# Softmax of the node scores: from TensorE transposes to VectorE's 32x32 blocks, with some steps of the pattern moved

## The chip, the core and the metric

The kernel runs on one core of a Trainium2 chip. A core has TensorE (PE in the profile: matmuls, which take a 128-row weight tile and stream the other operand through it, into PSUM), VectorE (DVE), ScalarE (ACT), GpSimd (POOL) and SyncE (SP, which here only issues DMAs). Each engine works through its own queue in the order in which the program wrote it, and waits at an instruction until the semaphores it needs have been counted up. The metric is the device time of one execution in microseconds, lower is better.

## The reference, cut to what matters

64 graphs of 256 nodes with 512 features. Layer 0 is three graph convolutions, layer 1 one graph attention whose softmax runs over the 256 nodes of a graph; both end in a residual and a layer norm.

```python
# layer 0
def gcn(x, adj, W, b):
    return einsum('bnm,bmh->bnh', adj, einsum('bnf,fh->bnh', x, W)) + b
h = relu(gcn(x, adj, W1, b1)); h = relu(gcn(h, adj, W2, b2))
x = layernorm(x + gcn(h, adj, W3, b3))
# layer 1
q, k = split(x @ Wqk); v = x @ Wv
agg = einsum('bij,bjd->bid', adj, k * mask)
w = mask * sum(q * agg, -1) / sqrt(512)      # one score per node, [64, 256]
out = layernorm(x + softmax(w, axis=1)[:, :, None] * v)
```

All inputs and outputs are float32.

## The kernel before

The 64 graphs are worked on in 32 pairs (G = 2 graphs). The 256 nodes lie as NH = 2 halves of 128 partitions. Most matrix products are cut into 2x2 blocks and done in seven block products in place of eight; the generator `seven` (L110) issues them. It uses three PSUM banks: x takes product 1, is copied out by ScalarE (L118), takes product 6 on top, is copied again (L127), takes product 5 on top, is read by the add `c22`, and takes product 3 on top, which `c12` reads. Banks v and y take products 7 and 4, and 2; they are read by ScalarE (L132) and the adds `c21` and `c11`. Those adds are VectorE's `add` (L65), whose second operand is one of the copies. The sums and differences of blocks that feed the products are formed by GpSimd (`padd`, L68; `a_sums`, L275; `t_sums`, L350) or VectorE.

Six generators issue the work of a round of the outer loop, each for another pair:

- F (`front`): three times `support` (times W1, W2, W3, matmuls on L304) and twice `aggregate` (times the adjacency, L326, with relu on ScalarE, L329).
- S (`sums`): GpSimd's block sums for the next pair, the bias added to x (`x<-x,b3b`), and the four block sums of the adjacency (`aS`).
- B (`back`): the third aggregation (`adj_times`, L362), residual and layer norm of layer 0. It starts with `t_sums`, GpSimd's four sums of the blocks that the last `support` left (`T<-sup`, `T<-sup,T`).
- G (`gather`): adjacency times the masked result (L362).
- M (`attention`): the scores, from products against a matrix that is formed once from Wq, Wk and Wv (L542). The operand `ring` is fetched anew from memory for every pair, seven blocks ahead. `results(g)` ends a graph: two scores on VectorE (L559, one for each half of the nodes: a product with the gathered rows, summed into one column of `w`), and a sum `v<-R`. `results(1)` comes before the last products of M, `results(0)` after them.
- E (`finish`): the softmax (`softmax_rows`, `softmax_cols`), the weighted residual (L600), statistics and layer norm, and the store.

In what order the generators are stepped stands written out: a letter of ORDER is one step of that generator. START and LAST do so for the first and the last pair, END for what is left after it; in END, X and Y are E for the last pair, graph by graph. All engines' queues follow from this one order. At each step an engine's instructions are put behind what is already in its queue.

The softmax before: the scores `w` are [128, 2, 2], nodes on partitions. TensorE transposes both halves into one bank, [2, 256] (L381); VectorE takes the maximum (L383), ScalarE the exponential with its sum (L386), VectorE the reciprocal and the scaling (L388, L389). In E's second step TensorE transposes back (L396), VectorE copies to SBUF (L398), and four operations form residual plus softmax times v (L600). The scale 1/sqrt(512) is in `mask_s`, which the scores use.

Of the kernel before, what the change touches and what calls it, by code (L numbers as in the profile page):

```python
# [9 lines left out]
FP = mybir.dt.float32  # L10
AF = mybir.ActivationFunctionType
OP = mybir.AluOpType
AX = mybir.AxisListType

P = 128
PAIR = 2
G = PAIR
# [3 lines left out]
def gcn_then_graph_attention(ctx: ExitStack, tc: tile.TileContext, xT, xN, adjT, mask, W1, b1, W2, b2, W3, b3,  # L21
# [18 lines left out]
    nc = tc.nc  # L40
    NPAIR = xT.shape[0]
    N, D = 256, 512
    NH, DC = N // P, D // P
    HD = D // 2
    EPS = 1e-5
    ISCALE = 1.0 / math.sqrt(D)
    KEYS = ("T1", "T2", "T3", "T4")

    const = ctx.enter_context(tc.tile_pool(name="const", bufs=1))
    pool = ctx.enter_context(tc.tile_pool(name="work", bufs=1))  # L50
    small = ctx.enter_context(tc.tile_pool(name="small", bufs=2))
# [6 lines left out]
    def bank(shape=(P, G, N)):  # L58
        return psum.tile(list(shape), FP, name="ps", tag="ps")
# [110 lines left out]
    ident = const.tile([P, P], FP, name="ident")  # L170
# [16 lines left out]
    for n, b in ((1, b1), (2, b2)):  # L187
        t = const.tile([P, DC], FP, name=f"b{n}")
# [1 line left out]
        bcol.append(t)  # L190
    b3b = const.tile([P, D], FP, name="b3b")
    mask_t = const.tile([P, NH, NPAIR * G], FP, name="mask_t")
    mask_s = const.tile([P, NH, NPAIR * G], FP, name="mask_s")
    eps = const.tile([P, 1], FP, name="eps")
    nc.vector.memset(eps, EPS)

    def prepare():

        for n, w in ((2, W2), (3, W3)):
            begin, end = load_w(w, n)  # L200
            begin()
            yield from end()
        aTs[1] = load_adj(1)
        nc.sync.dma_start(b3b, b3.partition_broadcast(P))
        nc.sync.dma_start(mask_t, mask.rearrange("p (h b) -> p h b", h=NH))
        yield
        nc.vector.tensor_scalar(mask_s, mask_t, ISCALE, None, op0=OP.mult)
        yield from make_m()


# [6 lines left out]
    for k in STEPS:  # L217
        q = "abcd".index(k)
# [154 lines left out]
        nc.vector.scalar_tensor_tensor(nb, mvt[:, :, :, 0], -1.0, rs, op0=OP.mult, op1=OP.mult)  # L373
        return rs, nb

    def softmax_rows(w, gs):

        n = len(gs)
        pw = bank((n, N))
        for h in range(NH):  # L380
            nc.tensor.transpose(pw[:, h * P:(h + 1) * P], w[:, h, gs[0]:gs[0] + n], ident)  # L381
        nmax = small.tile([n, 1], FP, name="nmax")
        nc.vector.tensor_reduce(nmax, pw, AX.X, OP.max, negate=True)  # L383
        e = small.tile([n, N], FP, name="e", bufs=1)
        tot = small.tile([n, 1], FP, name="tot")
        nc.scalar.activation(e, pw, AF.Exp, bias=nmax, accum_out=tot)  # L386
        rtot = small.tile([n, 1], FP, name="rtot")
        nc.vector.reciprocal(rtot, tot)  # L388
        nc.vector.tensor_scalar(e, e, rtot, None, op0=OP.mult)  # L389
        return e  # L390

    def softmax_cols(sm, gs):
        n = len(gs)
        ps = bank((P, NH, n))
        for h in range(NH):
            nc.tensor.transpose(ps[:, h, :], sm[:, h * P:(h + 1) * P], ident[:n, :n])  # L396
        s = small.tile([P, NH, n], FP, name="s", bufs=2)
        nc.vector.tensor_copy(s, ps)  # L398
        return s


# [25 lines left out]
    def back(i, C, aS, x, end, put):  # L427
# [20 lines left out]
        b = i * G  # L448
# [56 lines left out]
                        aTs[i + 2] = load_adj(i + 2)  # L505
                yield
        put["G"] = gather()
        w = small.tile([P, NH, G], FP, name="w", bufs=2)
        put["M"] = attention(i, x1b, w, r, put)

    def attention(i, x1b, w, r, put):

        half = lambda n, s: pool.tile([P, 4 - s, 4, P], FP, name=n, tag=f"{n}{'ab'[s]}", bufs=1)
        Z = [half("Z", s) for s in range(2)]
        I = [pool.tile([P, 4, 4 - s, P], FP, name="I", tag=f"I{'ab'[s]}", bufs=1) for s in range(2)]
        zo = lambda o: Z[o // 4][:, o % 4]
        z = lambda n: zo(place[n]).rearrange("p (c g) n -> p c g n", c=2)
        sub = OP.subtract
        for n, b in ((1, x1b(0, 0)), (2, x1b(0, 1)), (4, x1b(1, 1))):
            nc.scalar.copy(z(n), b)  # L520
        for o, a, b, op in ((z(5), x1b(1, 0), x1b(1, 1), OP.add), (z(6), z(5), z(1), sub), (z(7), z(1), x1b(1, 0), sub),
                            (z(3), z(2), z(6), sub)):
            nc.vector.tensor_tensor(o, a, b, op=op)  # L523
        yield
        for s in range(2):
            padd(I[s][:, 2], Z[s][:, :, 0], Z[s][:, :, 1], sub)
            padd(I[s][:, 0], Z[s][:, :, 1], Z[s][:, :, 3])
            padd(I[s][:, 1], I[s][:, 0], Z[s][:, :, 0], sub)
            padd(I[s][:, 3], Z[s][:, :, 2], I[s][:, 1], sub)
            yield  # L530
        left = {n: (lambda o, k=k: zo(o)[:, k]) for n, k in ((1, 0), (2, 2), (4, 3))}
        left.update({n: (lambda o, k=k: I[o // 4][:, k, o % 4]) for n, k in ((5, 0), (6, 1), (7, 2), (3, 3))})
        at = [i * len(uses)]

        def inner(q, R, more=None):

            outer = OUTER[q]

            def mm(n, ps, first):
                wt = ring.pop(at[0])  # L540
                for k, o in enumerate(outer):
                    nc.tensor.matmul(ps[:, k], lhsT=left[n](place[o]), rhs=wt[:, k], start=(first and k == 0),  # L542
                                     stop=(k == len(outer) - 1), skip_group_check=True)
                fetch(at[0] + RING)
                at[0] += 1
            if more is None:
                c12, plus = lambda x: nc.scalar.copy(R[:, :, 0, 1], x), None
            else:
                c12 = lambda x: add(R[:, :, 0, 1], x, more[:, :, 0, 1])
                plus = (more[:, :, 0, 0], more[:, :, 1, 0], more[:, :, 1, 1])  # L550
            return seven(mm, (P, len(outer), HD), lambda y, t: add(R[:, :, 0, 0], y, t), c12,
                         lambda v, t: add(R[:, :, 1, 0], v, t), lambda v, t: add(R[:, :, 1, 1], v, t), plus=plus)
        v = pool.tile([P, G, NH, D], FP, name="v", tag="v", bufs=1)
        flat = lambda R: R.rearrange("p g j f -> p g (j f)")

        def score(R, h, g):
            t = put["gt"][:, h, g, :]
            b = i * G + g
            nc.vector.scalar_tensor_tensor(t, R[:, g].rearrange("p j f -> p (j f)"), mask_s[:, h, b:b + 1], t,  # L559
                                           op0=OP.mult, op1=OP.mult, accum_out=w[:, h, g:g + 1])  # L560

        def results(g):

            score(C[:, 0], 1, g)
            yield
            score(B[:, 0], 0, g)
            yield
            add(v[:, g, 1], flat(C[:, 0])[:, g], flat(C[:, 1])[:, g])
            put[g] = r, v, w
            yield  # L570

        R = {k: pool.tile([P, 2, G, 2, HD], FP, name="R", tag=t, bufs=1) for k, t in (("a", "T"), ("b", "x1T"))}
        A, B = R["a"], R["b"]
        run = {k: inner("ab".index(k), R[k]) for k in "ab"}
        for n, k in enumerate(STEPS):
            if n == 14:
                add(B[:, 0], B[:, 0], A[:, 0])
                yield
                nc.vector.tensor_tensor(B[:, 0], B[:, 0], B[:, 1], op=sub)  # L579
                yield  # L580
                add(v[:, :, 0], flat(A[:, 0]), flat(A[:, 1]))
                yield
                C = pool.tile([P, 2, G, 2, HD], FP, name="R", tag="Za", bufs=1)
                run.update(c=inner(2, C, B), d=inner(3, B[:, :1], B[:, :1]))
            if n == 26:
                yield from results(1)
            next(run[k])
            yield
        yield from results(0)

    def finish(i, prev, gs=range(G)):

        r, v, w = prev
        n = len(gs)
        sm = softmax_rows(w, gs)
        yield
        s = softmax_cols(sm, gs)
        for k, g in enumerate(gs):
            for h in range(NH):
                nc.vector.scalar_tensor_tensor(v[:, g, h], v[:, g, h], s[:, h, k:k + 1], r[:, g, h, :],  # L600
                                               op0=OP.mult, op1=OP.add)
        yield
        st = small.tile([P, NH, n, 6], FP, name="st")
# [10 lines left out]
        for k, g in enumerate(gs):  # L614
            for h in range(NH):
# [4 lines left out]

    ORDER = ("BFEFFFEBFBEFBBBFBBFBBFFFBFBESBEFBBGFFGEFEEGEGFFEFESFFGMMGSFEMGMMFMMMMMMMMMMMMMMMMMFM"
             "MMMMMSFMMMSSMMSMSSFMFSMFMMEMSMMFM")
    START = ("FBBFBFFFBBFBBBFBBFBBBBFBFFBBBBBBFBBFBBBBBBBBFFFFBBFBBBBBBFFBBSBFFBFBBSFBBBFFSBBBFSBB"
             "BBSBFBSBFBSSSSBSBBBSBBB")
    LAST = ("BFEFFFEBFBEFBBBFBBFBBFFFBFBESBEFBBGFFGEFEEGEGFFEFESFFGMMGSFEMGMMFMMMMMMMMMMMMMMMMMFM"
            "MMMMMSFMMMSSMMSMSSFMFSMFMMEMSMMFM")
    END = ("EEBEBEBEEBBBEEEBBBEEBBBBBBGMGMGBGMMBMEMMMMMGGMMMBMMMMGMMMMMMMMMMMMMMMMMMXMXMMMMXMMYM"
           "XMXXMXMYMYYYXXYYMMXXMYXYYYY")  # L630

    def run(order, rest, **gens):
        res = {}
# [77 lines left out]
```

## Time and profile before

| | |
|---|---|
| median of 3 runs | 2789.59 us (2786.75 to 2791.51) |
| the profiled execution's own time | 2780.69 us |
| its span, from first to last instruction | 2778.9 us |
| granted TensorE clock | 0.994 |
| busy: TensorE / weight loads / VectorE / ScalarE / GpSimd | 98 / 86 / 62 / 41 / 65 % of the span |
| L381, first transposes on TensorE | 66 matmuls, 13.0 us busy |
| L396, transposes back | 66 matmuls, 9.4 us busy |
| L383, L388, L389, L398 on VectorE | 33 of each; 412, 151, 1206, 151 ns mean |
| L386 exponential on ScalarE | 33; 465 ns mean, and 185 for its sum |
| L559 scores on VectorE | 128; 1425 ns mean, 740 to 1747 |

Times in a profile line are microseconds unless ns is written. In the timeline, a line is a start, a duration, engine, source line, operation, output<-inputs, their shapes and how many were merged; in brackets the idle time before it and what ended it. Durations of matmuls overlap, since they are pipelined; the distance between starts is what they cost. The same is true in part for VectorE: the next operation is shown to start some 0.08 us before the end of the one before. The time of an operation includes a wait for the memory ports. The listing by line gives for each operation the minimum, median and maximum in ns, and the first and last start.

### The profile page before, as it was taken

How to read it: one execution, taken by the hardware profiler on the slowest of the kernel's cores; microseconds unless marked ns; L12 is line 12 of the kernel's file. 1: busy time of each engine (PE TensorE's matmuls, PEld its weight loads, DVE VectorE, ACT ScalarE, POOL GpSimd, SP SyncE). 2: the span in 40 equal slices, each digit the busy share in tenths (PEclk: the TensorE clock that was granted, in tenths of full speed). 3: DMA queues.
4: the chain of work that ended last, by engine and by line, in shares of the span. 5: the costliest groups of instructions: out<-in, count | busy, mean ns of one | idle time of the engine just before them, and what ended most of it. 6: DMA issues, size and time to landing. Idle time of an engine off the chain costs nothing.

```text
span 2778.9 us, 37024 instructions
## 1 busy us (share of the span) xinstructions
PE 2731.4 (98%) x12688; PEld 2377.9 (86%) x12688; DVE 1723.4 (62%) x2900; ACT 1143.7 (41%) x1890; POOL 1795.9 (65%) x1446
## 2 busy tenths in 40 slices
PE   9999999999999999999999999999999999999996
PEld 8888888888888888888888888888888888888875
DVE  4566565665566665656666666655566655666666
ACT  3334344434444433444334444334443334443434
POOL 3666765676756666656667666767566676667663
PEclk9999999999999999999999999999999999999997
DMA  6444554344554345543445543455444455434442
GB/s 223 153 122 131 163 174 136 113 146 150 162 166 130 118 139 169 161 148 125 134 139 161 171 134 116 139 161 161 154 126 127 139 161 173 137 112 145 139 153 97
DMA packets 197752, 403.45 MB, mean 145 GB/s; under 512 B 20160, under 2 KB 57408, under 8 KB 189504
## 3 DMA queue, kind: packets, MB, share of 16 engines
q1 hardware_dynamic: 197568, 401.10, 45.8%
q8 instruction: 103, 1.69, 0.3%
q14 instruction: 81, 0.66, 0.1%
HBM read 328.54 MB, written 72.48 MB: 144 GB/s over the span
## 4 chain that ended last, share of the span: by engine, by line
PE 93%; DMA 3%; DVE 2%; issue 1%; POOL 1%; ACT 0%; SPq 0%; POOLq 0%; ACTq 0%; DVEq 0%
PE ps L304 41%; PE ps L542 22%; PE ps L326 16%; PE ps L362 14%; DMA ring<-mv 3%; PE ps L246 1%; DVE v L600 0%; DVE gt L559 0%; PE ps L381 0%; PE ps L396 0%; DMA xT<-in_xT 0%; DVE R L65 0%; POOL S L286 0%; POOL tmp L68 0%; DVE st L607 0%
## 5 line engine op out<-in xcount | busy, mean ns | idle before, releaser
L304 PE MATMUL ps<-w_T,S 128*128 128x256 f32 x2304 | 539.7, 379 | 3.8 <-POOL S L287 2.8
L304 PEld LDWEIGHTS ps<-w_T,S 128*128 128x128 f32 x2304 | 435.1, 190 | 63.9 <-POOL S L287 4.0
L326 PE MATMUL ps<-aT,sup 128*128 128x256 f32 x2048 | 457.7, 379 | 0.0
L65 DVE TENSOR_TENSOR R<-ps,tmp 128x512 f32<-128x512 f32 (+1 forms) x384 | 230.5, 622 | 365.5 <-PE ps L542 350.3
L542 PE MATMUL ps<-ring,I 128*128 128x256 f32 x1792 | 428.5, 381 | 13.3 <-DMA ring<-mv 13.1
L326 PEld LDWEIGHTS ps<-aT,sup 128*128 128x128 f32 x2048 | 389.0, 190 | 52.8
L283 POOL TENSOR_TENSOR S<-hT 128x512 f32<-128x512 f32 x64 | 81.7, 1277 | 492.1 <-ACT hT L329 492.1
L542 PEld LDWEIGHTS ps<-ring,I 128*128 128x128 f32 x1792 | 339.7, 190 | 64.7 <-issue 15.1
L127 ACT COPY tmp<-ps 128x512 f32<-128x512 f32 (+1 forms) x288 | 158.0, 560 | 446.7 <-PE ps L542 183.8
L65 DVE TENSOR_TENSOR sup<-ps,tmp 128x512 f32<-128x512 f32 x288 | 197.4, 686 | 211.6 <-PE ps L304 211.6
L542 PE MATMUL ps<-ring,Z 128*128 128x256 f32 x1344 | 321.6, 379 | 0.0
L68 POOL TENSOR_TENSOR tmp<-tmp,R 128x512 f32<-128x512 f32 (+1 forms) x192 | 213.1, 1137 | 160.2 <-DVE R L579 141.2
L542 PEld LDWEIGHTS ps<-ring,Z 128*128 128x128 f32 x1344 | 255.4, 190 | 34.7
L307 ACT COPY sup<-ps 128x512 f32<-128x512 f32 x96 | 56.2, 585 | 457.1 <-PE ps L304 303.6
L68 POOL TENSOR_TENSOR I<-Z 128x384 f32<-128x384 f32 (+1 forms) x128 | 177.7, 1409 | 100.6 <-DVE Z L523 97.1
L304 PE MATMUL ps<-w,hT 128*128 128x256 f32 x1024 | 241.9, 379 | 0.0
L118 ACT COPY tmp<-ps 128x512 f32<-128x512 f32 (+1 forms) x288 | 158.8, 563 | 172.1 <-PE ps L304 86.0
L304 PEld LDWEIGHTS ps<-w,hT 128*128 128x128 f32 x1024 | 194.6, 190 | 26.4
L329 ACT ACTIVATE hT<-ps,b 128x512 f32<-128x512 f32 x256 | 171.3, 681 | 98.6 <-PE ps L326 96.9
L68 POOL TENSOR_TENSOR tmp<-tmp,x 128x512 f32<-128x512 f32 x96 | 120.5, 1270 | 128.7 <-ACT tmp L132 128.4
L65 DVE TENSOR_TENSOR gt<-ps,tmp 128x512 f32<-128x512 f32 x96 | 65.4, 682 | 222.6 <-PE ps L362 222.6
L68 POOL TENSOR_TENSOR x<-x,b3b 128x512 f32<-128x512 f32 x128 | 202.3, 1600 | 0.0
(111 smaller groups left out, 4755.0 us busy)
## 6 DMA issues: line engine op xcount, KB each, us to landing
ring<-mv SPq DMA_DIRECT2D x672, 256.0 KB, 3.5
x<-in_xN SPq DMA_DIRECT2D x32, 1024.0 KB, 6.0
out<-v SPq DMA_DIRECT2D x64, 512.0 KB, 2.7
xT<-in_xT SPq DMA_DIRECT2D x31, 1024.0 KB, 4.8
via<-tr SPq DMA_DIRECT2D x31, 1024.0 KB, 4.3
x1T<-via SPq DMA_DIRECT2D x124, 256.0 KB, 4.7
ring<-mv SPq DMA_DIRECT2D x224, 128.0 KB, 2.9
aT<-in_adjT SPq DMA_DIRECT2D x32, 512.0 KB, 3.5
```

The costliest lines, as they stand in the source:

```text
L65: nc.vector.tensor_tensor(o, a, b, op=OP.add)
L68: nc.gpsimd.tensor_tensor(o, a, b, op=op)
L118: nc.scalar.copy(t1, x)
L127: nc.scalar.copy(u, x)
L246: nc.tensor.matmul(pt[:, j * P:(j + 1) * P], lhsT=wq[:, d, f * P:(f + 1) * P], rhs=wk[:, d, j * P:(j + 1) * P], start=(d == 0 and j == 0), ...
L283: eng.tensor_tensor(S[2], blk(0, 0), blk(1, 0), op=sub)
L304: nc.tensor.matmul(ps[:, g], lhsT=src[n][:, c, g], rhs=w[n][:, c], start=(first and g == 0 and c == 0), stop=(g == G - 1 and c == 1), skip ...
L307: steps = seven(mm, (P, G, HD), lambda y, t: add(C[0][0], y, t), lambda x: nc.scalar.copy(C[0][1], x), lambda v, t: add(C[1][0], v, t), la ...
L326: nc.tensor.matmul(ps[:, g], lhsT=C[k][c // 2][:, g, (c % 2) * P:(c % 2 + 1) * P], rhs=aT[:, k, g], start=(g == 0 and k == 0), stop=(g == ...
L329: nc.scalar.activation(hT[c // 2][:, c % 2], ps, AF.Relu, bias=b[:, c:c + 1])
L362: nc.tensor.matmul(ps[:, g], lhsT=aS[n][:, g], rhs=mov[n][:, g], start=(first and g == 0), stop=(g == G - 1), skip_group_check=True)
L542: nc.tensor.matmul(ps[:, k], lhsT=left[n](place[o]), rhs=wt[:, k], start=(first and k == 0), stop=(k == len(outer) - 1), skip_group_check= ...
```

## The change

The scores of both graphs go to a tile that is kept, `scores` [128, 2, 32], of which two columns in each block of 32 are used. VectorE turns it in 32x32 blocks; a graph's scores then stand in one partition of each of four groups of 32 partitions, and four small operations bring them to partitions 0 and 1, multiplying by 1/sqrt(512) on the way. Maximum, exponential and scaling follow in the shape [2, 256]; four small copies and another block transpose bring the weights back to the nodes. TensorE has no part in it, and E's second step no longer waits for TensorE. The scores use `mask_t` without the scale. At the end of the program, X and Y each treat both graphs' rows and use one of them. ORDER, LAST and END are rewritten.

```diff
+    scores, turned, back_t = (const.tile([P, NH, 32], FP, name=n) for n in ("scores", "turned", "back"))
+    for t in (scores, back_t):
+        nc.gpsimd.memset(t, 0.0)
...
-        nc.vector.tensor_scalar(mask_s, mask_t, ISCALE, None, op0=OP.mult)
...
-    def softmax_rows(w, gs):
-        n = len(gs)
-        pw = bank((n, N))
-        for h in range(NH):
-            nc.tensor.transpose(pw[:, h * P:(h + 1) * P], w[:, h, gs[0]:gs[0] + n], ident)
-        nmax = small.tile([n, 1], FP, name="nmax")
-        nc.vector.tensor_reduce(nmax, pw, AX.X, OP.max, negate=True)
-        e = small.tile([n, N], FP, name="e", bufs=1)
-        tot = small.tile([n, 1], FP, name="tot")
-        nc.scalar.activation(e, pw, AF.Exp, bias=nmax, accum_out=tot)
-        rtot = small.tile([n, 1], FP, name="rtot")
+    def softmax_rows(w):
+        nc.vector.transpose(turned, w)
+        e = small.tile([G, NH, 4, 32], FP, name="e", bufs=1)
+        for q in range(4):
+            nc.vector.tensor_scalar(e[:, :, q], turned[q * 32:q * 32 + G], ISCALE, None, op0=OP.mult)
+        nmax = small.tile([G, 1], FP, name="nmax")
+        nc.vector.tensor_reduce(nmax, e, AX.XYZ, OP.max, negate=True)
+        tot = small.tile([G, 1], FP, name="tot")
+        nc.scalar.activation(e, e, AF.Exp, bias=nmax, accum_out=tot)
+        return e, tot
+
+    def softmax_cols(e, tot):
+        rtot = small.tile([G, 1], FP, name="rtot")
         nc.vector.reciprocal(rtot, tot)
         nc.vector.tensor_scalar(e, e, rtot, None, op0=OP.mult)
-        return e
-
-    def softmax_cols(sm, gs):
-        n = len(gs)
-        ps = bank((P, NH, n))
-        for h in range(NH):
-            nc.tensor.transpose(ps[:, h, :], sm[:, h * P:(h + 1) * P], ident[:n, :n])
-        s = small.tile([P, NH, n], FP, name="s", bufs=2)
-        nc.vector.tensor_copy(s, ps)
+        for q in range(4):
+            nc.vector.tensor_copy(back_t[q * 32:q * 32 + G], e[:, :, q])
+        s = small.tile([P, NH, 32], FP, name="s", bufs=1)
+        nc.vector.transpose(s, back_t)
         return s
...
-    ORDER = ("BFEFFFEBFBEFBBBFBBFBBFFFBFBESBEFBBGFFGEFEEGEGFFEFESFFGMMGSFEMGMMFMMMMMMMMMMMMMMMMMFM"
-             "MMMMMSFMMMSSMMSMSSFMFSMFMMEMSMMFM")
+    ORDER = ("BFEEFFFBFBEFBBBFBBFBBFFFBFBFSEBEBBGFFGEFEGFEEGEFFESGFFMMMSFGEGMMFMMMMMMMMMMMMMMMMMFM"
+             "MMMMMSFMMMSSMMMSSSMMFFMSMMEMFMSFM")
...
-    END = ("EEBEBEBEEBBBEEEBBBEEBBBBBBGMGMGBGMMBMEMMMMMGGMMMBMMMMGMMMMMMMMMMMMMMMMMMXMXMMMMXMMYM"
-           "XMXXMXMYMYYYXXYYMMXXMYXYYYY")
+    END = ("EEBBEBEEEBEBEBEBBBEEBBBBBBGGMGGMMBMMMGEMBBGMMMMMMMMMMMMMMMGMMMMMMMMMMMMMMXMMMMMXMYXX"
+           "YXXYMMYXYXMYMMMXMYXXMYYXYYY")
```

LAST is the same string as ORDER in both kernels. What the strings move in the queues of a steady pair:

- At its head, E's second step stands right behind the first. Before, three steps of F (its products 7, 6 and 2, with the add `c11`) stood between them.
- At its end, before: score, score (graph 1), F's product 2 with `c11`, `v<-R`, F's product 5 with `c22`, the next product of M, F's product 4 with `c21`, the last product of M, score, score (graph 0), `v<-R`, F's product 3. After: score, score, `v<-R`, the next product of M, F's products 2 and 5 with `c11` and `c22`, the last product of M, score, score, `v<-R`, F's product 4 with `c21`, F's product 3.
- In the middle: in the second `support`, F's product 4 goes ahead of G's product 2, and ScalarE's third normalisation of E ahead of the copy of F's product 3; G's product 5 goes from behind the third part of the second `aggregate` to behind its first, and G's product 4 from ahead of the fourth part to behind it; GpSimd's second group of four I sums goes ahead of three S sums.

More of the change, by code (lines that the diff above doesn't have):

```diff
@@ L192, in gcn_then_graph_attention @@
     mask_t = const.tile([P, NH, NPAIR * G], FP, name="mask_t")
-    mask_s = const.tile([P, NH, NPAIR * G], FP, name="mask_s")
     eps = const.tile([P, 1], FP, name="eps")
     nc.vector.memset(eps, EPS)
+    scores, turned, back_t = (const.tile([P, NH, 32], FP, name=n) for n in ("scores", "turned", "back"))
+    for t in (scores, back_t):
+        nc.gpsimd.memset(t, 0.0)
     def prepare():
@@ L507, in back @@
         put["G"] = gather()
-        w = small.tile([P, NH, G], FP, name="w", bufs=2)
-        put["M"] = attention(i, x1b, w, r, put)
+        put["M"] = attention(i, x1b, scores, r, put)
     def attention(i, x1b, w, r, put):
@@ L558, in score @@
             b = i * G + g
-            nc.vector.scalar_tensor_tensor(t, R[:, g].rearrange("p j f -> p (j f)"), mask_s[:, h, b:b + 1], t,
+            nc.vector.scalar_tensor_tensor(t, R[:, g].rearrange("p j f -> p (j f)"), mask_t[:, h, b:b + 1], t,
                                            op0=OP.mult, op1=OP.mult, accum_out=w[:, h, g:g + 1])
@@ L594, in finish @@
         n = len(gs)
-        sm = softmax_rows(w, gs)
+        sm = softmax_rows(w)
         yield
-        s = softmax_cols(sm, gs)
+        s = softmax_cols(*sm)
         for k, g in enumerate(gs):
             for h in range(NH):
-                nc.vector.scalar_tensor_tensor(v[:, g, h], v[:, g, h], s[:, h, k:k + 1], r[:, g, h, :],
+                nc.vector.scalar_tensor_tensor(v[:, g, h], v[:, g, h], s[:, h, g:g + 1], r[:, g, h, :],
                                                op0=OP.mult, op1=OP.add)
@@ L619, in finish @@
             nc.sync.dma_start(out[i, :, g * NH * D:(g + 1) * NH * D].rearrange("p (h f) -> p h f", h=NH), v[:, g])
-    ORDER = ("BFEFFFEBFBEFBBBFBBFBBFFFBFBESBEFBBGFFGEFEEGEGFFEFESFFGMMGSFEMGMMFMMMMMMMMMMMMMMMMMFM"
-             "MMMMMSFMMMSSMMSMSSFMFSMFMMEMSMMFM")
+    ORDER = ("BFEEFFFBFBEFBBBFBBFBBFFFBFBFSEBEBBGFFGEFEGFEEGEFFESGFFMMMSFGEGMMFMMMMMMMMMMMMMMMMMFM"
+             "MMMMMSFMMMSSMMMSSSMMFFMSMMEMFMSFM")
     START = ("FBBFBFFFBBFBBBFBBFBBBBFBFFBBBBBBFBBFBBBBBBBBFFFFBBFBBBBBBFFBBSBFFBFBBSFBBBFFSBBBFSBB"
              "BBSBFBSBFBSSSSBSBBBSBBB")
-    LAST = ("BFEFFFEBFBEFBBBFBBFBBFFFBFBESBEFBBGFFGEFEEGEGFFEFESFFGMMGSFEMGMMFMMMMMMMMMMMMMMMMMFM"
-            "MMMMMSFMMMSSMMSMSSFMFSMFMMEMSMMFM")
-    END = ("EEBEBEBEEBBBEEEBBBEEBBBBBBGMGMGBGMMBMEMMMMMGGMMMBMMMMGMMMMMMMMMMMMMMMMMMXMXMMMMXMMYM"
-           "XMXXMXMYMYYYXXYYMMXXMYXYYYY")
+    LAST = ("BFEEFFFBFBEFBBBFBBFBBFFFBFBFSEBEBBGFFGEFEGFEEGEFFESGFFMMMSFGEGMMFMMMMMMMMMMMMMMMMMFM"
+            "MMMMMSFMMMSSMMMSSSMMFFMSMMEMFMSFM")
+    END = ("EEBBEBEEEBEBEBEBBBEEBBBBBBGGMGGMMBMMMGEMBBGMMMMMMMMMMMMMMMGMMMMMMMMMMMMMMXMMMMMXMYXX"
+           "YXXYMMYXYXMYMMMXMYXXMYYXYYY")
     def run(order, rest, **gens):
```

## The prediction

> **What bounds the kernel now.** I read the page's busy row and chain first, then the timeline of one steady pair (about 85 us; here the one whose second half begins at 1000 us) by engine.
>
> ```profile
> PE 2731.4 (98%) x12688; PEld 2377.9 (86%) x12688; DVE 1723.4 (62%) x2900; ACT 1143.7 (41%) x1890; POOL 1795.9 (65%) x1446
> PE 93%; DMA 3%; DVE 2%; issue 1%; POOL 1%; ACT 0%; SPq 0%; POOLq 0%; ACTq 0%; DVEq 0%
> ```
>
> TensorE sets the end: eight 128x256 matmuls start every 1.72 us almost without a gap. So an edit is worth what it does to TensorE's stream, directly or by making it wait. The timeline of TensorE round the last product of a `support` (L304 reading `w,S`) and round the four transposes:
>
> ```profile
> 1000.70 1.89 PE L304 MATMUL ps<-w,hT 128*128 128x256 f32 x8
> 1002.42 1.89 PE L304 MATMUL ps<-w_T,S 128*128 128x256 f32 x8
> ...
> 1006.74 0.59 PE L542 MATMUL ps<-ring,I 128*128 128x256 f32 x2
> 1007.31 1.96 PE L304 MATMUL ps<-w,S 128*128 128x256 f32 x8
> ...
> 1009.97 1.89 PE L304 MATMUL ps<-w,xT 128*128 128x256 f32 x8
> 1011.70 0.38 PE L381 MATMUL ps<-ident,w 128*2 128x128 f32 x2
> ```
>
> Two matmuls from 1006.74 take 0.43 us of TensorE's time at that rate, up to 1007.17, but the next starts at 1007.31: the only repeated wait in this stretch, 0.14 us. Its cause stands in VectorE's timeline:
>
> ```profile
> 1001.48 1.73 DVE L559 SCALAR_TENSOR_TENSOR gt<-R,mask_s,gt 128x512 f32<-128x512 f32 x1
> ...
> 1003.14 1.74 DVE L559 SCALAR_TENSOR_TENSOR gt<-R,mask_s,gt 128x512 f32<-128x512 f32 x1
> ...
> 1004.81 0.68 DVE L65 TENSOR_TENSOR sup<-ps,tmp 128x512 f32<-128x512 f32 x1
> 1005.42 1.14 DVE L65 TENSOR_TENSOR v<-R 128x512 f32<-128x512 f32 x1
> 1006.48 0.68 DVE L65 TENSOR_TENSOR sup<-ps,tmp 128x512 f32<-128x512 f32 x1
> 1007.08 0.67 DVE L65 TENSOR_TENSOR R<-ps,R 128x512 f32<-128x512 f32 x1
> 1007.68 0.68 DVE L65 TENSOR_TENSOR sup<-ps,tmp 128x512 f32<-128x512 f32 x1
> ```
>
> The `sup` add of 1006.48 ends at 1007.16; it is `c22`, which must have read bank x before product 3 may accumulate into it, and product 3 follows 0.15 us later. So `c22` of the third `support` already has no slack. Why VectorE is late there shows in GpSimd's timeline and in the rows of the small operation L389:
>
> ```profile
> 1002.62 5.07 POOL L68 TENSOR_TENSOR x<-x,b3b 128x512 f32<-128x512 f32 x3
> ...
> 1011.40 2.94 POOL L97 TENSOR_TENSOR T<-sup 128x512 f32<-128x512 f32 x2
> 1014.42 2.61 POOL L97 TENSOR_TENSOR T<-sup,T 128x512 f32<-128x512 f32 x2
> ```
>
> ```profile
> L389 DVE TENSOR_SCALAR e<-e,rtot x33: 341/1259/1343, 167.1 to 2768.1; 2x256 f32<-2x256 f32 x31, 1x256 f32<-1x256 f32 x2
> ```
>
> Scores take 1.73 us here and 0.74 at the end of the program, where GpSimd is idle; L389 takes 0.34 alone and 1.26 beside GpSimd's `T` sums; one GpSimd sum takes 1.27 alone, 1.69 here. The two engines take turns.
>
> **What the skill says.** The Trainium skill, "SBUF — State Buffer", section "Who interferes with whom": VectorE and GpSimd share one port pair as an exclusive lock; a VectorE operation with two SBUF inputs, or a copy or tensor_scalar in a two-port mode, waits for GpSimd's whole instruction, a reduce never. The trace agrees (scores, `v<-R`, L389 wait; `sup<-ps,tmp`, with one input in PSUM, takes 0.68 always). "VectorE: DVE Perf Modes", section "The perf-mode tier table": fp32 copy and tensor_scalar from SBUF run at 2x, which is the two-port mode; L389 shows it for tensor_scalar, no row here for an SBUF copy. Same page, "The three transpose paths": VectorE turns 32x32 blocks only. L484 does this beside GpSimd in 0.60 us for 256 columns, no slower than alone.
>
> **The change, part by part.**
>
> *Transposes off TensorE.* From 1009.97 to the next eight, at 1011.92, are 1.95 us instead of 1.72: the first two transposes cost 0.22; the second two, by the same reading (1015.37 to 1017.40, 2.03 us), 0.30. Gain 0.52 us x 30 steady pairs = 15.6 us.
>
> *The moved end of the pair, the main term.* In the new pattern the F steps that issue `c11`, `c22` stand after the M steps that finish graph 1. VectorE's queue becomes score, score, `v<-R`, `R<-ps,R`, `c11`, `c22`, then the last `R`, score, score, `v<-R`, `c21`, softmax. TensorE's work between the moment that lets the scores start and product 3 is the same, reordered. Before, `c11` (0.61) ran while GpSimd held the port, and `v<-R` waited for it anyway. Now `v<-R` is issued at 1004.81, but GpSimd's second `x<-x,b3b` is already waiting and takes the pair until about 1006.0; so `v<-R` still gives way to its successor at 1006.48. Behind it now stand `R` (0.60), `c11` (0.60) and `c22` (0.68) instead of `c22` alone: it ends at 1008.36 instead of 1007.16, and product 3 starts 1.20 us later. Queued behind product 3 is all of TensorE. 1.20 x 31 pairs = +37.2 us. If VectorE had slack this would cost nothing; the 0.14 us wait says it has none. `R<-ps,R` and both pairs of scores keep their times, since the displaced `c21` (0.60) balances; `c21`'s result is wanted only by the fourth `T` sum and a matmul near 1022.
>
> *Softmax on VectorE.* Transpose of 64 columns, about 0.3 us (L484: 0.60 for 256), four tensor_scalars, reduce 0.41, exp 0.65 with its accumulator read, reciprocal 0.15, L389's scaling 0.34, four copies, transpose, four L600 at 0.67. A small operation is 0.15 us by L388, L398; if it takes both ports and GpSimd is busy, it waits out one GpSimd sum, 1.27. The first four fall on the four `T` sums, which end at 1013.1, 14.4, 15.8, 17.1, so the fourth ends near 1017.3, the reduce at 1017.8, the exp at 1018.4. Below: 0.6 us for the four; above: 5.2. I take the upper end, because L389 showed it for the same kind and type. Behind the exp on ScalarE stands the copy of F's product 6 (L127), done near 1018.95; product 5, due at 1018.9 after the 1.20 and less the 0.52, waits for it: about 0.2 us, between 0 and 0.5. x 30 = +6 (0 to 15). The copies come when GpSimd has at most one sum ready: 0.6 us. `c11` then comes near 1022.4 instead of 1017.3, `c22` at 1023.7, while its product 3 is due at 1026.0; the back stage's `c22` ends at 1026.4 for 1027.7. This delay is covered by 2.3 and 1.3 us; without the cover it would cost its own length.
>
> *Other moved steps.* F, G and S steps in the middle: no TensorE instruction comes nearer to its source than its wait allows (product 4 and the product after it swap; the second half of the I sums goes ahead of the S sums, wanted 13 us later). SP's issues keep their order but for one ring load. Zero; cover gone, at most 0.4 us a pair. `mask_s` gone: 0.22 us before the pairs, hidden under TensorE.
>
> *The end.* TensorE no longer waits 2.1 and 3.5 us for the softmax near 2703 to 2707, but VectorE is what the last back stage waits for, and the four small operations fall again on the `T` sums (2703.8 to 2709.8): `c11` of `r` comes near 2717.1 instead of 2715.0, and its successors likewise. The tail after the last score loses the transposes' round trips and gains eight small operations twice: about +0.5. Together +2 (minus 6 to plus 5).
>
> Sum: -15.6 + 37.2 + 6 + 2 = +29.6 us. The profiled execution took 2780.7 us (span 2778.9, 1.8 around it), giving 2810.3; the median of the runs is 8.9 above that execution, so the forecast is 2819.
>
> **Rivals.**
>
> *The add gets the port first (ends faster).* If VectorE, issuing `v<-R` just as its score lets go, is served before GpSimd's waiting sum, `v<-R` ends at 1005.4 and `c22` at 1007.2, product 3 starts as before: -15.6 + 2 to 6, about 2780. It decides when `v<-R` is done by 1005.3. Against it: in every pair of scores the second waits for the sum that had queued up. 11 in 100.
>
> *The small operations don't lock.* The first four cost 0.6: the exp is early, product 5 doesn't wait, the end gains 2 to 4 us: -15.6 + 37.2 - 2, about 2809. For it: 64 elements over two partitions is a form without a row. 24 in 100.
>
> *VectorE's lag reaches further.* If the copies and scaling lock too and meet `tmp<-tmp,x` (2.6 us more), the 2.3 and 1.3 us of cover are gone and a product 3 waits about 0.7 us: +20, about 2839. 13 in 100.
>
> **How the numbers follow.** Main case 52 in 100 (2812 to 2829). The range 2796 to 2846 leaves out the first rival and the far ends. A difference under 0.2% (5.6 us) can't be told from none. Faster is the first rival: 0.11; same, a main stall half as long with nothing else, 0.03; slower 0.86.
>
> **What would show it.** Product 3 of the third `support` should wait about 1.3 us in each pair, released by a `sup` add; no L381 or L396 on TensorE; the four tensor_scalars near 1.3 us each, the copies near 0.15; exp some 5 us later, ScalarE waiting for the reduce. The forecast is wrong if `v<-R` is short behind the scores, or if that matmul doesn't wait.

## The result, and the profile after

The changed kernel takes 2832.97 us (median of 4 runs, 2829.73 to 2834.81); the kernel before took 2790.55 us beside it (4 runs, 2786.75 to 2794.76). The ratio is 1.015, 95% interval 1.0133 to 1.0168: slower by 42 us. The forecast was 2819, slower, in a range of 2796 to 2846. Direction and range hold, but 14 us are missing, and behind them stands a term of some 20 us that the forecast put at zero. It is the subject of most of what follows.

First the page after, its busy row and its chain:

```profile
PE 2715.8 (96%) x12556; PEld 2371.0 (84%) x12556; DVE 1870.2 (66%) x3196; ACT 1134.1 (40%) x1890; POOL 1791.4 (63%) x1448
PE 75%; POOL 13%; DMA 7%; DVE 2%; issue 2%; ACT 1%; SPq 0%; POOLq 0%; ACTq 0%; DVEq 0%
```

TensorE has 132 instructions fewer (12688 before), exactly the transposes, and is busy 15.6 us less, yet the span grew by 52.3 us, from 2778.9 to 2831.2. The chain says by what kind of wait: it ran through TensorE for 93% before, for 75% now; DMA rose from 3% to 7%, and GpSimd from 1% to 13%. The two waits are named by TensorE's table of waits (what was waited for, us in total, times, longest). After:

```profile
PE ps L541 <- DMA ring<-mv: 37.3, 29, 2.9
PE ps L306 <- POOL aS L68: 35.9, 31, 1.2
```

And before, where the second row does not exist:

```profile
PE ps L542 <- DMA ring<-mv: 13.1, 13, 1.5
```

So two waits came: one in every pair at a product of `support` (L306, before L304), and one for the attention's weight blocks (`ring`), which was there in 13 pairs, and is there in nearly all now.

**The wait at `support`.** This is TensorE's timeline after, round the last product of the third `support` (`w,S`):

```profile
1021.13 0.59 PE L541 MATMUL ps<-ring,I 128*128 128x256 f32 x2
1021.56 1.89 PE L306 MATMUL ps<-w_T,hT 128*128 128x256 f32 x8
1024.61 1.97 PE L306 MATMUL ps<-w,S 128*128 128x256 f32 x8 [1.16 <-POOL aS L68]
```

Eight matmuls from 1021.56 at 1.72 us are started up by 1023.28, but the next starts at 1024.61: 1.33 us of waiting where there were 0.14 (the row's own 1.16 counts from the modelled end of the matmul before). VectorE's timeline over the same time:

```profile
1019.25 1.74 DVE L558 SCALAR_TENSOR_TENSOR gt<-R,mask_t,gt 128x512 f32<-128x512 f32 x1
...
1020.93 1.74 DVE L65 TENSOR_TENSOR v<-R 128x512 f32<-128x512 f32 x1
1022.59 0.68 DVE L65 TENSOR_TENSOR R<-ps,R 128x512 f32<-128x512 f32 x1
1023.19 1.27 DVE L65 TENSOR_TENSOR sup<-ps,tmp 128x512 f32<-128x512 f32 x2
```

That is the order of the new pattern: score, `v<-R`, `R`, `c11`, `c22`. Beside it GpSimd runs three sums back to back:

```profile
1018.74 5.06 POOL L68 TENSOR_TENSOR x<-x,b3b 128x512 f32<-128x512 f32 x3
```

The second of them ends at 1022.12, and `v<-R`, shown from 1020.93, only 0.55 us after it. So the sum went ahead, as the forecast had it, and `v<-R` takes 1.74 us, in all 31 pairs. The pair `c11`, `c22` ends at 1024.46, and product 3 starts 0.15 us later, the distance it kept before as well. The page names GpSimd's `aS` sum as the releaser; that sum ended at 1024.48 and product 3 doesn't read it: two events at nearly one time, and the wrong one named, which is also why the chain gives GpSimd 13% (0% in the run below in which this wait is gone and the rest is as changed). The operation to look for is the one that the waiting matmul depends on, here the last reader of its bank.

**The softmax.** VectorE's timeline of the same pair:

```profile
1028.62 0.23 DVE L380 STREAM_TRANSPOSE turned<-scores 128x64 f32<-128x64 f32 x1
1028.89 3.00 DVE L383 TENSOR_SCALAR e<-turned 2x64 f32<-2x64 f32 x4
1031.92 0.41 DVE L385 TENSOR_REDUCE nmax<-e 2x1 f32<-2x256 f32 x1
...
1033.18 1.37 DVE L394 TENSOR_SCALAR e<-e,rtot 2x256 f32<-2x256 f32 x1
1034.59 0.78 DVE L396 COPY back<-e 2x64 f32<-2x64 f32 x4
1035.40 0.24 DVE L398 STREAM_TRANSPOSE s<-back 128x64 f32<-128x64 f32 x1
```

The four scalings take 3.0 us here, not the 0.8 that all four take at the end of the program, where GpSimd idles, and not the forecast's 5.2. TensorE's stream does not notice: its next product in this stretch, product 5 of the following `support` at 1035.05, follows its predecessor at the usual distance.

**The weight blocks.** SyncE's timeline, the issues of one pair, before (first) and after (second). Last in each, from TensorE's timeline, stands the product of that pair that waits; it needs the first block issued behind `x`:

```profile
971.86 0.34 SPq L84 DMA_DIRECT2D aT<-in_adjT  x1
975.27 1.18 SPq L228 DMA_DIRECT2D ring<-mv  x2
976.55 0.38 SPq L89 DMA_DIRECT2D x<-in_xN  x1
978.73 5.50 SPq L228 DMA_DIRECT2D ring<-mv  x7
985.08 1.10 PE L542 MATMUL ps<-ring,I 128*128 128x256 f32 x4 [1.21 <-DMA ring<-mv]
```

```profile
989.81 0.34 SPq L84 DMA_DIRECT2D aT<-in_adjT  x1
991.50 1.18 SPq L230 DMA_DIRECT2D ring<-mv  x2
992.77 0.38 SPq L89 DMA_DIRECT2D x<-in_xN  x1
994.95 5.50 SPq L230 DMA_DIRECT2D ring<-mv  x7
1001.20 1.10 PE L541 MATMUL ps<-ring,I 128*128 128x256 f32 x4 [1.09 <-DMA ring<-mv]
```

The adjacency load (512 KB, some 3.5 us to landing) stood 3.4 us ahead of the weight blocks, and was nearly done when they came; now it stands 1.7 us ahead, its second half runs together with the two weight blocks, and it lands 0.2 us behind the issue of `x` (1 MB) in place of 1.2 us ahead of it. By the page's table of issues `x` takes 6.0 us to landing before, 7.6 after, in the median. The pair of before shown here is one of the 13 that wait: in it `x` took 7.8 us too. In 11 of the 13 it took 7.1 to 8.0 us, in the steady pairs without a wait 5.3 to 6.6. So a late `x` is nothing new; with the later adjacency load it is the rule. What makes it late in those pairs of before stays open. The load waits for the last reader of the buffer it fills, which is G's product 4; and that product moved from ahead of the fourth part of the second `aggregate` to behind it, which is 1.72 us. That the DMA engines have no room left while TensorE waits shows in the longest of these waits of the changed kernel (TensorE's timeline, then a row of the windows: length, busy time of PE, PEld, DVE, ACT, POOL, clock, DMA share, GB/s):

```profile
1174.67 1.10 PE L541 MATMUL ps<-ring,I 128*128 128x256 f32 x4 [2.89 <-DMA ring<-mv]
```

```profile
1172.00:1174.70 2.70, 0.03 (x1) 0.06 (x1) 0.57 (x1) 0.00 (x0) 2.62 (x3) 1.00 1.02 387
```

The Trainium skill, "DMA: Bandwidth & Descriptors", section "Queues, rings and completion order", says that on each DMA engine descriptors are consumed in ring order; all these loads are issued on SyncE's queue, so a weight block waits for what stands ahead of it. The traces agree as far as they show it: in each of the two, all 1244 transfers landed in the order of their issue, and the engines are full (1.02 at 387 GB/s) while TensorE is idle.

**The balance.** The time from one third-support `w,S` to that of the next pair gives it cleanly. In pairs without a wait for `ring` it is 84.15 us before and 84.71 after (where only two pairs have none). Its mean over all 30 is 84.66 and 86.17, so the waits for `ring`, with what follows them, are 0.51 us a pair before and 1.46 after. Over 30 pairs: +17 for the pattern itself, +28.5 for `ring`. With 3.2 up to the first of these points (159.8 to 163.0 us) and 3.8 from the last to the end (79.2 to 83.0), that is the 52.3 us between the spans. The medians differ by 42 only: the profiled execution of before took 2780.7 us, 10 below the median beside it, the one of after was at its median. The waits for `ring` vary from one execution to the next, so the 28.5 is for these two executions; the runs below give 19 to 24.

### The profile page after: what moved, and what is told of

Same layout as the page of the kernel before. It is cut to its first block, busy times and chain, and to the rows that moved or that the text cites. A ratio compares the mean times of both kernels' runs of the same rounds, so it can differ in the third digit from the quotient of the medians.

```text
span 2831.2 us, 37026 instructions
## 1 busy us (share of the span) xinstructions
PE 2715.8 (96%) x12556; PEld 2371.0 (84%) x12556; DVE 1870.2 (66%) x3196; ACT 1134.1 (40%) x1890; POOL 1791.4 (63%) x1448
## 4 chain that ended last, share of the span: by engine, by line
PE 75%; POOL 13%; DMA 7%; DVE 2%; issue 2%; ACT 1%; SPq 0%; POOLq 0%; ACTq 0%; DVEq 0%
PE ps L306 33%; PE ps L328 15%; PE ps L364 13%; PE ps L541 13%; DMA ring<-mv 7%; POOL x L68 7%; POOL tmp L68 4%; POOL S L292 1%; POOL aS L68 1%; ACT tmp L132 1%; PE ps L248 1%; ACT tmp L127 0%; DVE gt L558 0%; DVE v L599 0%; DMA xT<-in_xT 0%
## 5 line engine op out<-in xcount | busy, mean ns | idle before, releaser
L306 PE MATMUL ps<-w_T,S 128*128 128x256 f32 x2304 | 539.6, 379 | 3.2 <-POOL S L289 1.8
L306 PEld LDWEIGHTS ps<-w_T,S 128*128 128x128 f32 x2304 | 437.4, 190 | 64.0 <-POOL S L289 3.1
L541 PE MATMUL ps<-ring,I 128*128 128x256 f32 x1792 | 432.2, 381 | 37.6 <-DMA ring<-mv 37.3
L65 DVE TENSOR_TENSOR sup<-ps,tmp 128x512 f32<-128x512 f32 x288 | 191.6, 682 | 132.9 <-PE ps L306 132.9
L306 PE MATMUL ps<-w,hT 128*128 128x256 f32 x1024 | 241.9, 379 | 0.0
L68 POOL TENSOR_TENSOR I<-Z 128x384 f32<-128x384 f32 (+1 forms) x128 | 172.0, 1363 | 77.9 <-ACT Z L519 77.2
L306 PE MATMUL ps<-w,S 128*128 128x256 f32 x768 | 183.8, 382 | 37.8 <-POOL aS L68 35.9
L306 PEld LDWEIGHTS ps<-w,hT 128*128 128x128 f32 x1024 | 194.6, 190 | 26.5
L364 PE MATMUL ps<-T,aS 128*128 128x256 f32 x768 | 198.3, 381 | 5.0 <-ACT tmp L118 3.1
```

The source lines that it names most:

```text
L65: nc.vector.tensor_tensor(o, a, b, op=OP.add)
L68: nc.gpsimd.tensor_tensor(o, a, b, op=op)
L306: nc.tensor.matmul(ps[:, g], lhsT=src[n][:, c, g], rhs=w[n][:, c], start=(first and g == 0 and c == 0), stop=(g == G - 1 and c == 1), skip ...
L364: nc.tensor.matmul(ps[:, g], lhsT=aS[n][:, g], rhs=mov[n][:, g], start=(first and g == 0), stop=(g == G - 1), skip_group_check=True)
```

## The experiments

Two questions. Of the moved steps, which one costs what? And what makes the weight blocks late? My theory: the end of the pattern costs the wait behind `c22`, the middle the late adjacency load, and the softmax itself gains. The rivals are with each run. Ratios are to the kernel before, run beside each on the same chip (2789.9, 2782.8 and 2779.8 us in the three batches); the expectations' absolute times start from 2790. Some expectations count the waits for `ring` from start to start of the matmuls: 44.6 us for the changed kernel, where the table of waits has 37.3. The waits of a run are those of its one profiled execution. The pattern's strings are cut with dots in the diffs; LAST changes with ORDER.

**The middle of the pattern put back.** The changed kernel, with the pattern's middle as before:

```diff
-    ORDER = ("...FSEBEBBGFFGEFEGFEEGEFFESGFFMMMSFGEGMM..."
+    ORDER = ("...ESBEFBBGFFGEFEEGEGFFEFESFFGMMGSFEMGMM..."
```

> The changed kernel with the middle of its pattern as before (G's products 5 and 4, the I and S sums), head, tail, END and softmax as changed. Theory: the waits of TensorE for ring, 37 us against 13 before, come from the moved G step, behind which the adjacency load stands; they go back to about 13 us and the time to 2808 us, while product 3 of the third support still waits 1.3 us in each pair. Rival: the ring waits follow from the late product 3, which shifts TensorE against the transfers; then nothing changes, 2833 us.

Measured: 2812.48 us, ratio 1.0082 (1.0062 to 1.0102), for 1.015: some 19 us come back. The waits for `ring` fall to 21.3 us, not to the 13 of the theory. A pair without a wait for `ring` still takes 84.70 us, and the row of L306 stays. So the middle's price lies in the waits alone.

**The end of the pattern put back.** The changed kernel with:

```diff
-    ORDER = ("...MSSSMMFFMSMMEMFMSFM")
+    ORDER = ("...SMSSFMFSMFMMEMSMMFM")
```

> The changed kernel with the end of its pattern as before (c11 and c22 between the scores and the products of M), head, middle, END and softmax as changed. Theory: product 3 of the third support starts 1.2 us earlier in each of 31 pairs, 38 us less, 2795 us; the ring waits stay near 37 us. Rival, the ring waits follow from the late product 3: 62 us less, 2771 us. Rival, the softmax on VectorE makes VectorE late there and not the order: less than 10 us.

Measured: 2801.28 us, ratio 1.0044 (1.0028 to 1.0061): some 30 us come back. The shortest pair falls from 84.71 to 83.52 us, by the 1.20 of the prediction, and the waits behind `c22` from 41.0 us in all (start to start, what exceeds the usual step) to 4.2. That is 36.8 us, of which 30 arrive: the waits for `ring` grow meanwhile, from 1.46 to 1.75 us a pair in the two traces (that of this run is its slowest of six executions, 2806 us).

**Both put back**, so that the softmax on VectorE remains, with E's second step behind its first, and the new order of the last iteration:

> The changed kernel with middle and end of the pattern as before; what is left of the change is the softmax on VectorE, with its two steps one behind the other, and END. Theory: the 15.6 us of the transposes are gained and about 4 us lost behind the last pair: 2779 us, faster than before. Rival, the softmax's small operations cost as much as they gain in each pair: 2790 us or more.

Measured: 2779.6 us, ratio 0.9962 (0.9949 to 0.9976): faster than before by about 10 us. Pairs without a wait for `ring` take 83.51 us, 0.64 less than before: that is what the transposes cost, less whatever the softmax on VectorE costs in a pair. Over 30 pairs it is 19 us, and less than that arrives, since the end is longer by 5 us (84.2 for 79.2) and the waits for `ring` take 0.92 us a pair in this execution.

**The kernel before with the new middle alone:**

```diff
-    ORDER = ("...ESBEFBBGFFGEFEEGEGFFEFESFFGMMGSFEMGMM..."
+    ORDER = ("...FSEBEBBGFFGEFEGFEEGEFFESGFFMMMSFGEGMM..."
```

> The kernel before, transposes on TensorE, with the changed middle of the pattern alone. Theory: the adjacency load is issued some 1.7 us later, ring blocks land later, TensorE waits for ring about 37 us instead of 13: 2815 us. Rival, the ring waits need the late product 3: no change, 2790 us.

Measured: 2812.11 us, ratio 1.0083 (1.0059 to 1.0107). The same 22 us without the new softmax, and in the table of waits the same row as after:

```profile
PE ps L542 <- DMA ring<-mv: 35.9, 27, 2.0
```

A pair without a wait is still 84.15 us, as before. The effect belongs to the middle, and doesn't depend on what else is changed.

**One step of the middle put back.** The changed kernel, in which G's product 4 alone goes ahead of the fourth part of the aggregate again:

```diff
-    ORDER = ("...FFMMMSFGEG..."
+    ORDER = ("...FFMMMSGFEG..."
```

> The changed kernel with one step put back: G's product of aT and T (product 4, the last reader of the adjacency buffer) stands ahead of the fourth part of the second aggregate again, as before. Theory (the adjacency load is issued one aggregate part, 1.72 us, later, and the weight blocks behind it land late): the load is issued some 13 us ahead of the first waiting block again, the waits for ring fall from 44.6 us to the 26 of the kernel with the whole middle put back, and the time from 2833 to about 2815. Rival (another of the moved steps of the middle, such as G's product 5 or the adds of the hidden state, makes the waits): stays at 2833.

Measured: 2798.51 us, ratio 1.0064 (1.0042 to 1.0085), which is 24 us less than the change and no worse than the whole middle put back. Waits for `ring` fall from 37.3 to 19.7 us in the slowest of its six executions (2813 us):

```profile
PE ps L541 <- DMA ring<-mv: 19.7, 16, 2.0
```

So of the middle's moves this one carries the price.

**The load of `x` later.** Is it `x` that the blocks queue behind? The changed kernel with:

```diff
-        put["x"] = load_x(i)
+        due.append(lambda: put.update(x=load_x(i)))
...
+            if n == 13 and due:
+                due.pop()()
             next(run[k])
```

> The changed kernel with the load of x (1 MB) issued eleven attention products later, past the weight blocks of the first half. Theory (the weight block that TensorE waits for is the one issued right behind x and the adjacency load, and queues behind their 1.5 MB): the waits for ring fall from 44.6 us to under 10, and the time from 2833 to about 2798. Rival (the transfers as a whole are the limit there, so that the wait only moves to a block further on): 2825 to 2840.

And the same on the kernel with middle and end put back, with the third `support`'s `c11` and `c22` both ahead of `v<-R`:

```diff
-    ORDER = ("...SMSSFMFSMFMMEMSMMFM")
+    ORDER = ("...SMSSFFMSMFMMEMSMMFM")
```

> The softmax on VectorE with the middle and the end of the pattern as before (2779.6), the load of x issued eleven products later, and the adds c11 and c22 of the third support both ahead of the add into v. Theory: the ring waits of 29.5 us fall to under 10 (-20 to -25), and the 0.13 us wait of product 3 goes (-4): about 2753. Rival (the transfers are the limit, and the add into v delays the scores of the next graph instead): 2775 to 2785.

Measured: 2843.83 us, ratio 1.0233 (1.0199 to 1.0267), and 2810.73, ratio 1.0099 (1.0077 to 1.0121). Both are worse than either theory had. The old wait is gone from the first half of the attention, as the theory says, and a longer one stands where `x` now is. TensorE's and SyncE's timelines of the second:

```profile
999.45 2.75 PE L544 MATMUL ps<-ring,I 128*128 128x256 f32 x12
1004.37 1.63 PE L544 MATMUL ps<-ring,Z 128*128 128x256 f32 x6 [2.17 <-DMA ring<-mv]
```

```profile
996.13 0.42 SPq L89 DMA_DIRECT2D x<-in_xN  x1
996.65 4.67 SPq L231 DMA_DIRECT2D ring<-mv  x5
```

In all it waits 53.3 us for `ring`, in 31 pairs. At both places tried, the block issued behind `x` is the one that is late; neither place within the attention was free for 1 MB. What did work is the order of the adds: the wait behind `c22` is 0.0 us in this run (4.2 in the kernel with both put back).

**The scalings on ScalarE**, which, the Trainium skill says ("SBUF — State Buffer", "Who interferes with whom"), shares no port with GpSimd; on the kernel with both put back:

```diff
-            nc.vector.tensor_scalar(e[:, :, q], turned[q * 32:q * 32 + G], ISCALE, None, op0=OP.mult)
+            nc.scalar.mul(e[:, :, q], turned[q * 32:q * 32 + G], ISCALE)
```

> The softmax on VectorE with the middle and the end of the pattern as before (2779.6), and the four scalings of the turned scores on ScalarE, [...]instead of VectorE. Theory (the wait of every second scaling for a T sum is hidden in the pairs and counts only at the end): the exp comes 1 to 2 us earlier, ring and product waits as they were, 0 to -3 us: 2777 to 2780. Rival (the late exp holds up ScalarE's copies and by them TensorE in every pair, as the forecast had it with 0.2 us): -6 us, 2774 or less. Against both: ScalarE's four operations stand ahead of its copies of TensorE's results and cost more than they save: 2785 or more.

Measured: 2771.65 us, ratio 0.9961 (0.9946 to 0.9976), the ratio of the kernel that it starts from (0.9962). Each takes 0.25 us in the median, beside GpSimd too, and the exp starts 2.8 us after the transpose instead of 4.3; a pair without a wait for `ring` stays at 83.51 us, the end at 84.2. So those 1.5 us of the exp cost nothing in this kernel, in the pairs or at the end.

**The adjacency load out of the way.** It is wanted some 20 us after the attention products at the earliest. The changed kernel with nothing but:

```diff
-                        aTs[i + 2] = load_adj(i + 2)
+                        due.append(lambda: aTs.update({i + 2: load_adj(i + 2)}))
...
+            if n == 24 and due:
+                due.pop()()
             next(run[k])
```

> The changed kernel with nothing but the load of the adjacency blocks (512 KB, wanted 20 us after the attention products at the earliest) issued at the 25th attention product instead of ahead of the first. Theory (the waits for ring come from 1.5 MB, adjacency and x, standing ahead of the weight block, and 0.5 MB less is enough to end them): the waits for ring fall from 44.6 us to under 10, the 41 us of the product behind c22 stay, time 2833 to about 2797, 1.001 to 1.005 of before. Rival (x alone, 1 MB, holds the weight block up, as the run with the late x suggests, where the wait moved with x): 2815 or more.

Measured: 2798.28 us, ratio 1.0064 (1.0044 to 1.0084), 24 us less than the change. The waits for `ring` are back to what before had, 12.7 us in 12 pairs, not under the 10 of the theory:

```profile
PE ps L542 <- DMA ring<-mv: 12.7, 12, 1.6
```

What the change added there is gone; a rest remains. The same edit on the kernel before tells whose that is:

> The kernel before with nothing but the adjacency load at the 25th attention product. Theory (the load also causes the 16.7 us of ring waits that the kernel before has): -13 to -17 us, 0.9945 of before. Rival (x alone): within 5 us of before.

Measured: 2778.58 us, ratio 0.9994 (0.998 to 1.0007; 12 runs against 15), no difference, with 15.2 us of waits for `ring` in 12 pairs. My theory falls here: the waits that the kernel before has do not come from the adjacency load. The rival, that `x` alone makes them, fits, since the waits moved with `x` in the two runs above; no run took `x` out of the attention, so it is not shown. Of the three places for the adjacency load, early and late take the same time; only the one between, close to `x`, costs.

**The best of these together**: softmax on VectorE with its scalings on ScalarE, the middle as before, `c11` and `c22` ahead of `v<-R`, the adjacency load late.

> The softmax on VectorE with its four scalings on ScalarE, the middle of the pattern as before, c11 and c22 both ahead of the add into v, and the adjacency load at the 25th attention product. From the kernel with the scalings on ScalarE (2771.7, ring waits 21.4 us, 4.1 us of waits behind c22). Theory: both waits go, -20 to -25: about 2749, 0.988 of before. Rival (x alone holds the ring up): 2765 to 2770.

Measured: 2755.7 us, ratio 0.9911 (0.9887 to 0.9935), faster than both kernels. A pair without a wait takes 83.31 us. Its page:

```profile
PE 2702.2 (98%) x12556; PEld 2372.8 (86%) x12556; DVE 1787.8 (65%) x3064; ACT 1175.2 (43%) x2022; POOL 1810.5 (66%) x1448
PE 94%; DMA 2%; DVE 2%; issue 1%; POOL 1%; ACT 1%; SPq 0%; POOLq 0%; ACTq 0%; DVEq 0%
```

It stayed above the theory's 0.988 because a wait for `ring` remains (8.8 us in 8 pairs). It goes with `x` again: in the seven pairs with a wait over 0.9 us `x` took 7.5 to 8.2 us to landing, in the other steady pairs at most 6.4.

**The same with the order of the last iteration as before:**

> The run above with the order of the last iteration (END) as before. Theory (the end is longer by 4 to 5 us because the softmax's small operations stand in VectorE's queue, not by its order): the stretch from the last product behind c22 to the end stays within 1.5 us of 84, time as the run above within 2 us. Rival (the new order of the end costs the 4 to 5 us): the stretch falls to about 80, time 4 us under the run above.

Measured: 2757.41 us, ratio 0.9923 (0.9898 to 0.9948), the same as the last run within the intervals. But the stretch from the last product behind `c22` to the end is 87.8 us, against 84.5 with the new order. Both theories are wrong: the new order neither costs the end anything nor leaves it alone; with the softmax on VectorE it saves 3.3 us of it, in one execution each. What of the softmax makes the end some 5 us longer than before's 79.2 was not settled: the four scalings aren't it.

## Why the prediction was right or wrong, step by step

- *"Transposes off TensorE", -15.6: right, a little small.* Measured 0.64 us a pair, not 0.52: -19. The reading of the two gaps left out what follows the second one: the first two matmuls of `T,aS` stand 0.32 us apart there before, 0.10 more than usual. A cost of the softmax in the pair, if there is one, is contained in the 0.64.
- *"The moved end of the pair, the main term", +37.2: right in mechanism and size.* Product 3 waits 1.33 us in the pair shown, where the forecast adds 1.20 to the 0.14 that was there; the end put back takes 1.20 us out of the shortest pair. In the time it is 30 to 33 us (with the middle new, and with it as before), since the weight blocks take a part of such a gain back.
- *"Softmax on VectorE", +6: wrong, no cost was found.* The link that failed is the length of the four scalings: 3.0 us for 5.2, because the first waits only for the rest of a GpSimd sum and the third for none. The copy of F's product 6, behind the exp, was then done at 1033.43 us in the pair shown, 1.6 us before product 5 starts, so product 5 didn't wait; making the exp earlier still changed nothing. The delay on VectorE afterwards (`c11`, `c22` of the next `support`) was hidden by the cover given, as said.
- *"Other moved steps": "Zero; cover gone, at most 0.4 us a pair." This is the step that failed*: +19 to 24 us by the runs, 0.6 to 0.8 us a pair. It asked whether a TensorE instruction comes too near its source, and whether SyncE's issues keep their order. They do. But it didn't ask *when* they are issued: the adjacency load waits for G's product 4, that product moved by 1.72 us, and 512 KB came to lie beside the weight blocks and `x`. The run that moved this load alone, out of their way, got the 24 us back.
- *"The end", +2: measured +3.8*, inside the bounds given.
- *The rivals.* "The add gets the port first" is refuted by the 1.74 us of `v<-R` in every pair. "The small operations don't lock" is half true (3.0 us lies between 0.8 and 5.2), but its time, 2809, rests on the same zero for the moved steps. "VectorE's lag reaches further" came nearest in time, 2839, for a wrong reason: no product of the next `support` waits.

By the runs the parts add up: the softmax alone -0.4% (2779.6 for 2789.9), the middle +0.8%, the end +1.1 to 1.2%, together the measured 1.5%. That the forecast came within 14 us was luck in part: three terms were too high (+6 for 0, -15.6 for -19, +37.2 for the 30 to 33 that arrived) and stood against one of some 20 us that was missing.

## What to carry to other kernels

When an instruction moves, look up which DMA waits for it to free a buffer, and draw that transfer into the timeline of transfers at its new place: the issue order can be unchanged, and the load still slide into a stretch where the queue is full. A large load with slack belongs, as here, ahead of or behind the stretch in which small blocks are consumed as they land; moving `x` within that stretch only moved the wait. And in a queue of short operations, those with a bank that TensorE waits for go ahead of one that may have to give way to another engine.

## What the runs showed that I had not expected

Small VectorE operations beside GpSimd don't each wait for a whole sum. In a steady pair the four `TENSOR_SCALAR e<-turned` take 389, 1214, 182 and 1167 ns (medians over the pairs): the first waits for the rest of the sum that is running, the second and fourth for a whole one, and the third slips in before the next sum starts, at the price it has alone. The copies of the same shape take 182 to 187 ns in the median; only single ones wait (1256 ns at most). That is a matter of when they come: in the run with the scalings on ScalarE they come earlier, and the first two take 1152 and 1214 ns in the median.

In the trace of the changed kernel, after two of the long waits for `ring` (2.3 and 2.6 us from start to start) the next 8 and 6 steps between matmuls were 0.40 to 0.43 us instead of 0.215. Others as long were not followed by this, nor was the longest, 3.3 us. The granted clock shows why. These are rows of the windows (columns as in the row shown above), two round the wait of 2.6 us, then two round the longest:

```profile
1773.63:1777.04 3.41, 1.29 (x6) 0.78 (x5) 1.77 (x3) 0.59 (x1) 3.33 (x4) 1.00 1.02 386
1777.04:1780.46 3.42, 3.31 (x8) 2.71 (x9) 0.69 (x1) 0.00 (x0) 1.64 (x2) 0.50 0.40 123
1169.47:1172.89 3.42, 2.31 (x11) 1.70 (x9) 2.08 (x3) 1.47 (x3) 3.26 (x4) 1.00 0.89 299
1172.89:1176.30 3.41, 1.63 (x8) 1.48 (x9) 0.42 (x1) 0.00 (x0) 2.65 (x3) 1.00 0.69 257
```

The clock stood at 0.50 for 3.413 us. The two such stretches of this trace among the pairs begin at 138.646 and 1777.043 us, which is 480 times 3.4133 us apart, so the span is divided here into windows of that length. The wait of 2.6 us fell almost wholly into one window; the longest was split over two. Over the fourteen traces, from 160 to 2660 us, 15 windows had a stretch at 0.50 right behind them, and in each of them TensorE had stood without a matmul for 2.07 us or more (counted from the starts, 0.215 us for each matmul). In the other 10 225 windows at full clock it was 2.07 us or less. So in these runs not the length of a wait decides but how much of one window it takes, with the border near 2.07 of 3.41 us. Six of the 15 are in the first run with the late `x` and four in the second; at 5 to 8 slow steps each, some 0.2 us a step, they are a part of why these two were worse than either theory.
